# A chain of Mamba, window and convolution layers on one core: the output y written over the conv's output, and three of twelve products with B moved to GpSimd in the second mixer stage

## The chip, the cores and the metric

One core of one Trainium2 chip runs the whole program in one launch. The metric is the device time of that launch in microseconds (us). Engines are named as in the profile: PE (TensorE matmul), PEld (its weight loads), DVE (VectorE), ACT (ScalarE), POOL (GpSimd), SP (SyncE, which issues nearly all DMAs).

## What is computed

An image batch of 4 x 192 x 64 x 64 in float32 goes through four layers. Layer 0 is a norm and two Mamba mixers (the second on flipped channels), added to the norm's output. Layer 1 is a norm, one Mamba mixer, a depthwise 3x3 conv with a GELU and an MLP. Layers 2 and 3 are a masked conv with generated weights and a window layer with two projections. The change concerns the mixers of layers 0 and 1 alone. A mixer, cut from the reference:

```python
xc, z = split(x @ in_w.T)
xc = silu(causal_conv(xc) + conv_b)
dt, B, C = split(xc @ x_w.T)
dt = softplus(dt @ dt_w.T + dt_b)
# for each step t, channel d (384) and state n (16):
h = exp(dt * A) * h + (dt * xc) * B
y = sum_n(h * C)
out = ((y + D * xc) * silu(z)) @ out_w.T
```

## The kernel before

**Stages.** `two_mambas` computes layer 0 (the first stage): 32 tiles of 512 tokens, each with two mixers m0 and m1, so 64 mixer tiles. `mamba_block` computes layer 1 (the second stage): 32 mixer tiles of 512 tokens with one mixer (`summed=True`), and beside them, on the same engines, the output projection, the depthwise conv, a norm and the MLP of earlier tiles. `conv_and_windows` follows.

**The scan.** A mixer tile has 12 groups k of 4 scan steps j, 48 steps in all. A group covers 4 x 128 rows (16 channels times 8 states each) by 512 tokens. For a group:

- SP loads dt and dt*xc, spread over the states, from DRAM to `dtE` and `dtxE` (`load`, L588), a pair of groups at a time and 8 or 12 steps ahead.
- The **product** with B (L616 to 626): h = dtxE * B, 128 x 2048 elements. B lies spread in a PSUM bank of its own (`spread`, L597), which DVE reads. [...] In the first stage `shared` is (3, 7, 11) for m0 and (2, 5, 8, 11) for m1. In the second it is empty.
- ACT makes the decay dA = exp(dt * A), one 128 x 512 per step, two steps ahead, in three PSUM banks (`decay`, L628).
- DVE scans (`step`, L634, L636).
- POOL copies the last column to `state` and multiplies h by C (`read`, L645 to 651), issued after the group's last step.
- PE sums over the states with a gather matrix, four 32-column matmuls side by side (`sum`, L653), some steps later.

After every third of the groups, `skip` and `gate` (L677 to 691) make y = (ys + D * xc) * silu(z). In the first stage D * xc is added by one more matmul (`skip_w`) and DVE multiplies by z. In the second DVE adds D * xc and POOL multiplies. y is a tile of its own, one per mixer, and the out projection in `back` reads it.

**What sets the order.** All instructions are put in order by hand, on the host. `Scans.run` goes through the steps of all tiles in a row. A step issues its loads, the decay of two steps later, its own scan, and at the group's end the read with C and the next product (L741 to 785); a shared product is issued six steps ahead of its first scan (L761). Sums, skips and gates fall due a fixed number of steps later (L776). After each step `behind.tick` adds the work that runs beside the scans. This work stands in lanes (`Behind`, L175): generators that yield a `Piece` with the PE time of the next piece, the ticks to wait, what must have been issued before, and whether it needs one of two PSUM banks. A tick gives 1.6 (first stage) or 1.8 (second) of PE time. An ACT copy out of a bank is put off by `later` for one or two ticks, a DVE read by two or three. A `burst` is a long ACT function that needs another table than the decay's exp (Silu, Softplus, Gelu): it goes out only at an **edge** (L737), one per edge, and an edge is a tick before a group whose product DVE makes. `force` (L270) issues everything until a condition holds, for example `"rows" in u` before the first load of a next tile (L751).

In the second stage a tile has five bursts: Silu of xc (L488), Softplus of dt (L512), Silu of z (L530), Gelu of the conv branch (L1136) and Gelu of the MLP (L388). Lane 1 holds the front half (in projection, taps, dt, z) of the next tile and then the norm of the one after it; lane 0 the spread of C and `back`; lanes 2 and 3 the conv, the second norm and the MLP.

Of the kernel before, what the change touches and what calls it, by code (L numbers as in the profile page):

```python
# [22 lines left out]
C = 192  # L23
# [151 lines left out]
class Behind:  # L175
# [7 lines left out]

    def __init__(self, psum, tile, act, dve, spare, lanes=4):
# [234 lines left out]
class Mamba:  # L419
# [3 lines left out]
    def __init__(  # L423
        self, nc, name, taps, ins, const, last, scan, work, psum_y, psum_a, dram, ident, ex, behind, shared=(),
        summed=False,
    ):

        self.behind, self.y_free, self.shared, self.summed = behind, True, shared, summed  # L430
# [24 lines left out]
        if shared:  # L455
            self.skip_w = scan.tile([128, ND, 128], F32, name=f"{name}_skip")
            for d in range(ND):
                nc.vector.tensor_scalar_mul(self.skip_w[:, d, :], ident, self.D[:, d : d + 1])
        self.halo = scan.tile([128, ND, taps if summed else taps - 1], F32, name=f"{name}_halo")
        self.state = scan.tile([128, NQ, 4], F32, name=f"{name}_state")  # L460

    def front(self, xn, first, u):
# [28 lines left out]
        for d in range(ND):  # L491
            nc.tensor.matmul(ps, self.x_w[:, d, :], xc[:, d, :], start=(d == 0), stop=(d == ND - 1))  # L492
        dbl = u["dbl"] = self.work.tile([RK + 2 * NS, T], F32, name="dbl", bufs=2)
        h = behind.later(lambda ps=ps: nc.scalar.copy(dbl, ps))  # L494
# [29 lines left out]
        for d in range(ND):  # L524
            if d:
                yield Piece(1.7, bank=True)
            made.append(project(ND + d, z[:, d, :]))
        u["xn_read"] = True
        yield Piece(after=made, burst=True, act=4.1)
        nc.scalar.activation(z, z, AF.Silu)  # L530
        u["silu"] = True

    def convolve(self, raw, project, u):
# [6 lines left out]
        for d in range(ND):  # L540
            for j in range(K):
                if j % 2 == 0:
                    yield Piece(1.7 if j < K - 1 else 0.85, bank=j == 0, after=made + u["xc_free"])
                if d == j == 0:
                    xc = u["xc"] = self.work.tile([128, ND, T], F32, name="xc", bufs=3)
                if j == 0:
                    ps = behind.bank([128, T], "ps_conv")
                nc.tensor.matmul(  # L548
                    ps, self.conv[:, d, j, :], raw[:, d, j : j + T], start=(j == 0), stop=(j == K - 1)
                )  # L550
# [10 lines left out]
    def sum_taps(self, raw, projected, u):  # L561
# [3 lines left out]
        for d in range(ND):  # L565
            yield Piece(1.7, bank=True, after=u["xc_free"])
            if d == 0:
                xc = u["xc"] = self.work.tile([128, ND, T], F32, name="xc", bufs=3)
                one = self.work.tile([128, ND, 1 + T], F32, name="one", tag="dt", bufs=1)
# [27 lines left out]
    def spread(self, u, o):  # L597

        B = u["B", o] = self.psum_a.tile([128, T], F32, name=f"B{o}", bufs=1)
        self.nc.tensor.matmul(B, self.ex.spread[:, o, :], u["dbl"], start=True, stop=True)  # L600

    def spread_C(self, u, o):

        for n, i in (("C", 2 + o), ("Bs", o)):
            if n == "Bs" and not any(k % 2 == o for k in self.shared):
                return
            if n == "Bs":
                yield Piece(0.85, bank=True)
# [44 lines left out]
    def sum(self, u, k):  # L653
# [3 lines left out]
        for j in range(4):  # L657
# [4 lines left out]
                start=(i == 0),  # L662
                stop=(i == 3 and not self.shared),
                skip_group_check=bool(self.shared),
            )
        if i == 3 and self.shared:
            c = k // 4
# [9 lines left out]
    def skip(self, u, c):  # L677
        if c == 0:
            u["y"] = self.last.tile([128, ND, T], F32, name=f"{self.name}_y", bufs=1)
        if self.shared:  # L680
            self.nc.vector.tensor_tensor(u["y"][:, c, :], u["ys"], u["z"][:, c, :], ALU.mult)
            return
        self.nc.vector.scalar_tensor_tensor(
            u["y"][:, c, :], u["xc"][:, c, :], self.D[:, c : c + 1], u["ys"], ALU.mult, ALU.add
        )

    def gate(self, u, c):
        if self.shared:
            return
        y = u["y"][:, c, :]  # L690
        self.nc.gpsimd.tensor_tensor(y, y, u["z"][:, c, :], ALU.mult)


class Scans:
# [6 lines left out]
    def __init__(self, nc, units, behind):  # L701
        self.nc, self.units, self.behind = nc, units, behind
        self.due = {}
        for n, unit in enumerate(units):
            unit[1]["skipped"], unit[1]["gated"] = [False], [False]
            unit[1]["xc_free"] = [units[n - 3][1]["skipped"]] if n > 2 else []
            unit[1]["z_free"] = [units[n - 2][1]["gated"]] if n > 1 else []
# [8 lines left out]
    def run(self):  # L716
# [3 lines left out]
        for o in range(2):  # L720
            m.spread(u, o)
            self.behind.add(0, m.spread_C(u, o), Piece(0.85, bank=True))
        for i in range(2):
# [17 lines left out]
    def step(self, i, n):  # L741
# [24 lines left out]
        if j == 3:  # L766
            self.behind.force(lambda: ("C", k % 2) in u)
            m.read(u, k)
            if k >= NQ - 2 and i + 8 < n:
                m2, u2, _, _ = self.tile(i + 8)  # L770
                self.behind.add(0, m2.spread_C(u2, k - (NQ - 2)), Piece(0.85, bank=True))
# [19 lines left out]
    def skip(self, m, u, c):  # L791
        self.behind.force(lambda: "silu" in u)
        if c == 0:
            self.behind.force(lambda: m.y_free)
            m.y_free = False
        m.skip(u, c)
        u["skipped"][0] = c == ND - 1

# [5 lines left out]
def two_mambas(tc, x, gb_ap, m_ins, ex_aps, out, at_first):  # L804
# [3 lines left out]
    with ExitStack() as ctx:  # L808
# [16 lines left out]
            Mamba(  # L825
                nc, f"m{i}", 4, m_ins[i], const, work, const, work, psum_y, psum_a, dram, ident, ex, behind, ((3, 7, 11), (2, 5, 8, 11))[i]
            )
# [51 lines left out]
        def back(u):  # L879
            o = work.tile([128, nq, C], F32, name="o", bufs=2)  # L880
            made = []
            for q in range(nq):
                yield Piece(2.6, bank=True, wait=0 if q else 2)
                ps = behind.bank([128, C], "ps_out")
                for i in range(2):
                    for d in range(ND):
                        nc.tensor.matmul(
                            ps,
                            u[i]["y"][:, d, bass.ts(q, 128)],
                            mambas[i].out_w[:, d, :],  # L890
# [13 lines left out]
                made.append(behind.later(lambda q=q, ps=ps: nc.scalar.copy(o[:, q, :], ps)))  # L904
            mambas[0].y_free = mambas[1].y_free = True
            yield Piece(after=made)
# [91 lines left out]
def mamba_block(tc, x, p96, p96_ap, p128, p128_ap, m_in, ex_aps, out, sums, following):  # L998
# [4 lines left out]
    with ExitStack() as ctx:  # L1003
# [57 lines left out]
        def back(u):  # L1061
# [13 lines left out]
            for k in range(2):  # L1075
                yield Piece(2.6, bank=True, wait=0 if k else 3)
                ps = behind.bank([CP, T], "ps_out")
                for d in range(ND):
                    nc.tensor.matmul(
                        ps,  # L1080
                        mamba.out_w[:, d, bass.ts(k, CP)],
                        u["m"]["y"][:, d, :],
                        start=(d == 0),
# [12 lines left out]
                )  # L1096
            mamba.y_free = True
            yield Piece(after=made)
# [734 lines left out]
```

## Time and profile before

| | us |
|---|---|
| three runs | 10616.35, 10621.16, 10621.92 (median 10621.16) |
| the profiled execution | 10617.22 |
| its span, first to last instruction | 10615.4 |
| first scan and last scan of the first stage, start | 77.4, 5236.6 |
| first scan and last scan of the second stage, start | 5337.7, 8693.0 |
| product with B on DVE (L623), mean | 2.262 |
| product with B on POOL (L623), mean | 4.645 |
| read with C on POOL (L649), mean | 4.533 |
| one scan (L636), mean | 1.267 |
| ACT copy of C or Bs (L612), median | 0.584, 0.586 |
| an ACT table load | 1.283 |

How to read it: the profile is one execution of the program. An engine's time is busy when one of its instructions runs; the idle time before an instruction is put down to what ended last before it started (the releaser). A mean over the whole program mixes the stages, so the views by stretch of time say more. The granted clock is the share of full speed at which PE was allowed to run; matmuls take longer where it is low.

### The profile page before, as it was taken

What the parts mean: (1) busy time and instruction counts of PE and PEld (TensorE: products, weight loads), DVE (VectorE), ACT (ScalarE), POOL (GpSimd) and SP (SyncE); (2) the same over time, 40 slices, a digit from 0 to 9 for tenths busy, and PEclk for the clock granted to TensorE, in tenths of its full rate; (3) what the DMA queues carried; (4) which work ended last, traced back from release to release, by engine and by line L of the source; (5) the groups of instructions that cost most, each with busy time, mean ns of one, the idle gap of its engine ahead of it and who ended that gap; (6) DMA issues with size and microseconds to landing.
All of it is one profiled execution on the core that took longest, in us unless ns stands there. A gap on an engine that the chain in (4) does not pass through costs nothing. (4 is left out here: it accounts for less than half of the span.)

```text
span 10615.4 us, 97365 instructions
## 1 busy us (share of the span) xinstructions
PE 8816.2 (83%) x30840; PEld 3533.1 (33%) x30840; DVE 8979.4 (85%) x7665; ACT 6664.2 (63%) x9658; POOL 7510.6 (71%) x3616
## 2 busy tenths in 40 slices
PE   6887887887877888888569999999999986889899
PEld 2322222322322322322223333333333333545555
DVE  7999999999999999999788888888888876555552
ACT  5676776667676767767456676767676653434433
POOL 6999999999999999999767777777777651111100
PEclk7888888888888888888668888898988887999999
DMA  6666666666666666666455555555555542122110
GB/s 167 172 185 182 179 182 186 179 179 185 182 181 183 182 181 183 183 182 179 132 147 142 140 143 141 143 141 147 141 143 141 142 103 73 45 52 60 44 41 18
DMA packets 969561, 1515.12 MB, mean 143 GB/s; under 512 B 244346, under 2 KB 277150, under 8 KB 968534
## 3 DMA queue, kind: packets, MB, share of 16 engines
q1 hardware_dynamic: 968190, 1505.85, 53.2%
q8 instruction: 244, 4.00, 0.2%
q10 hardware_dynamic: 856, 3.05, 0.1%
q14 instruction: 271, 2.22, 0.1%
HBM read 1295.45 MB, written 213.12 MB: 142 GB/s over the span
## 5 line engine op out<-in xcount | busy, mean ns | idle before, releaser
L636 DVE TENSOR_TENSOR_SCAN h<-dA,m_state,h 128x512 f32<-128x512 f32 x3712 | 4518.1, 1267 | 340.8 <-ACT dA L630 262.3
L649 POOL TENSOR_TENSOR h<-h,C 128x2048 f32<-128x2048 f32 x928 | 4206.4, 4533 | 75.1 <-POOL m_state L648 0.6
L630 ACT ACTIVATE dA<-dtE,m_A 128x512 f32<-128x512 f32 x4608 | 3105.4, 687 | 1446.1 <-DVE h L636 1328.3
L623 DVE TENSOR_TENSOR h<-dtxE,B 128x2048 f32<-128x2048 f32 x928 | 2099.0, 2262 | 78.0 <-DMA dtxE<-r_dtx 68.5
L658 PE MATMUL y<-h,gather 128*32 128x512 f32 x7424 | 1160.8, 701 | 462.0 <-POOL h L649 338.2
L1368 POOL TENSOR_TENSOR d<-d,rs 128x512 f32<-128x512 f32 x64 | 86.3, 1349 | 1597.1 <-DVE rs L1367 1576.5
L636 DVE TENSOR_TENSOR_SCAN h_apart<-dA,m_state,h_apart 128x512 f32<-128x512 f32 x896 | 1079.3, 1260 | 63.5 <-ACT dA L630 55.1
L474 PE MATMUL ps_in<-xT,m_in_w 96*128 96x512 f32 x1536 | 917.2, 746 | 244.6 <-ACT o L904 154.1
L623 POOL TENSOR_TENSOR h_apart<-dtxE,Bs 128x2048 f32<-128x2048 f32 x224 | 1040.5, 4645 | 10.0 <-ACT Bs L612 10.0
L649 POOL TENSOR_TENSOR h_apart<-h_apart,C 128x2048 f32<-128x2048 f32 x224 | 1014.6, 4529 | 18.0
L648 POOL COPY m_state<-h 128x4 f32<-128x4 f32 x928 | 176.8, 191 | 888.8 <-DVE h L636 883.8
L548 PE MATMUL ps_conv<-raw,m_conv 128*128 128x512 f32 x1536 | 724.2, 608 | 7.2 <-ACT raw L481 6.0
L474 PEld LDWEIGHTS ps_in<-xT,m_in_w 96*128 96x128 f32 x1536 | 357.9, 243 | 839.3 <-issue 373.3
L1117 PE MATMUL ps_dw<-strip,dw 96*96 96x512 f32 x1152 | 588.4, 660 | 3.3 <-ACT x L1126 0.9
L474 PE MATMUL ps_in<-xn,m_in_w 96*128 96x512 f32 x768 | 443.1, 721 | 164.4 <-ACT z L481 70.6
L658 PEld LDWEIGHTS y<-h,gather 128*32 128x32 f32 x7424 | 156.3, 115 | 1175.8 <-issue 580.9
L503 PE MATMUL ps_dt<-dbl,m_dt_w 12*128 12x512 f32 x576 | 410.4, 824 | 156.1 <-ACT dbl L494 99.5
L395 PE MATMUL ps_o<-hid,t 128*96 128x512 f32 x768 | 449.9, 733 | 78.7 <-ACT ln_rs L332 66.8
L1533 PE MATMUL sed_ps<-xn,sed 64*128 64x256 f32 (+3 forms) x2944 | 486.0, 404 | 7.0 <-DVE y L1552 7.0
L492 PE MATMUL ps_x<-xc,m_pack 128*44 128x512 f32 x576 | 357.6, 771 | 142.8 <-ACT xc L488 133.7
L630 ACT ACT_TABLE_LOAD x345 | 442.6, 1283 | 14.8 <-DMA dtE<-r_dt 8.6
L513 POOL TENSOR_TENSOR raw<-dt,xc 128x1536 f32<-128x1536 f32 x96 | 325.0, 3385 | 166.0 <-ACT dt L512 129.6
(202 smaller groups left out, 12347.7 us busy)
## 6 DMA issues: line engine op xcount, KB each, us to landing
dtE<-r_dt SPq DMA_DIRECT2D x2304, 256.0 KB, 5.2
dtxE<-r_dtx SPq DMA_DIRECT2D x2304, 256.0 KB, 4.2
r_dt<-dt SPq DMA_DIRECT2D x96, 768.0 KB, 4.0
r_dtx<-raw SPq DMA_DIRECT2D x96, 768.0 KB, 6.5
x<-x SPq DMA_DIRECT2D x64, 384.0 KB, 3.9
img<-x SPq DMA_DIRECT2D x28, 512.0 KB, 8.1
xt<-in_x SPq DMA_DIRECT2D x32, 384.0 KB, 5.4
x<-o SPq DMA_DIRECT2D x32, 384.0 KB, 3.9
```

The lines of the kernel that those rows point to most:

```text
L395: nc.tensor.matmul(ps, self.w2[:, m, bass.ts(k, CP)], h[:, m, :], start=(m == 0), stop=(m == NH - 1),)
L474: nc.tensor.matmul(ps, self.in_w[:, k, bass.ts(e, 128)], xn[:, k, :], start=(k == 0), stop=(k == 1))
L492: nc.tensor.matmul(ps, self.x_w[:, d, :], xc[:, d, :], start=(d == 0), stop=(d == ND - 1))
L503: nc.tensor.matmul(ps, self.dt_w[:, bass.ts(d, 128)], dbl[:RK, :], start=True, stop=True)
L548: nc.tensor.matmul(ps, self.conv[:, d, j, :], raw[:, d, j : j + T], start=(j == 0), stop=(j == K - 1))
L623: engine.tensor_tensor(h, u["rows", k // 2, 1], u[B, k % 2].unsqueeze(1).broadcast_to([128, 4, T]), ALU.mult)
L630: self.nc.scalar.activation(dA, u["rows", k // 2, 0][:, j, :], AF.Exp, scale=self.A[:, k, j : j + 1])
L636: self.nc.vector.tensor_tensor_scan(h[:, j, :], u.pop(("dA", k, j)), h[:, j, :], self.state[:, k, j : j + 1], ALU.mult, ALU.add,)
L649: nc.gpsimd.tensor_tensor(h, h, u["C", k % 2].unsqueeze(1).broadcast_to([128, 4, T]), ALU.mult)
L658: self.nc.tensor.matmul(u["ys"][32 * j : 32 * j + 32, :], self.ex.gather[:, i // 2, :], h[:, j, :], start=(i == 0), stop=(i == 3 and not s ...
L1117: nc.tensor.matmul(ps, dw[:, k, j, :], s[:, k, dy : dy + rows, dx : dx + HW], start=(j == 0), stop=(j == 8),)
L1533: nc.tensor.matmul(out, sed[p, int(h is not None), i ^ position(k, s), cols], xn[b, g][p, c, :], start=group(t) not in begun, stop=left[gr ...
```

## The change

In the mixers of both stages:

- y is no tile of its own: `skip` and `gate` write over xc, and the out projection reads xc. xc now lies in the pool of longer life (`last`), with three buffers in the second stage as before and four in the first (`xcs`). Instead of `skipped` and `y_free`, a flag `y_read` frees the buffer once the out projection is issued.
- `dbl` has one buffer instead of two.
- `Bs` is copied by ACT from B's own PSUM bank; the second matmul for it is gone.

In the second stage alone:

- `shared` is (3, 7, 11): POOL makes three of twelve products, into one `h_apart` buffer. With that, the ticks before groups 3, 7 and 11 are no edges.
- `spread_C` makes Bs first and C second for odd groups; for even groups C has one buffer and its matmul waits three ticks.
- Silu of z moves from lane 1 into a lane 4 of its own.
- The sum of groups 1, 5 and 9 comes one step later.

The core of the diff:

```diff
-        dbl = u["dbl"] = self.work.tile([RK + 2 * NS, T], F32, name="dbl", bufs=2)
+        dbl = u["dbl"] = self.work.tile([RK + 2 * NS, T], F32, name="dbl", bufs=1)
...
-        u["xn_read"] = True
-        yield Piece(after=made, burst=True, act=4.1)
-        nc.scalar.activation(z, z, AF.Silu)
-        u["silu"] = True
+        def silu():
+            nc.scalar.activation(z, z, AF.Silu)
+            u["silu"] = True
+            yield Piece()
+        said = Piece(after=made, burst=True, act=4.1)
+        if self.summed:
+            behind.add(4, silu(), said)
+        else:
+            yield said
+            yield from silu()
...
-                    xc = u["xc"] = self.work.tile([128, ND, T], F32, name="xc", bufs=3)
+                    xc = u["xc"] = self.last.tile([128, ND, T], F32, name="xc", bufs=self.xcs)
...
+    def alone(self, o):
+        return self.summed and o == 0
     def spread_C(self, u, o):
-        for n, i in (("C", 2 + o), ("Bs", o)):
-            if n == "Bs" and not any(k % 2 == o for k in self.shared):
-                return
-            if n == "Bs":
-                yield Piece(0.85, bank=True)
-            v = self.work.tile([128, T], F32, name=f"{n}{o}", bufs=2 if n == "C" else 1)
-            ps = self.behind.bank([128, T], f"ps_{n}")
-            self.nc.tensor.matmul(ps, self.ex.spread[:, i, :], u["dbl"], start=True, stop=True)
-            done = self.behind.later(lambda v=v, ps=ps: self.nc.scalar.copy(v, ps))
+        both = [("Bs", 0, 1)] if any(k % 2 == o for k in self.shared) else []
+        both.insert(len(both) if self.summed else 0, ("C", 2 + o, 1 if self.alone(o) else 2))
+        for n, i, bufs in both:
+            if n == "C":
+                yield Piece(0.85, bank=True, wait=3 * self.alone(o))
+            v = self.work.tile([128, T], F32, name=f"{n}{o}", bufs=bufs)
+            if n == "C":
+                ps = self.behind.bank([128, T], f"ps_{n}")
+                self.nc.tensor.matmul(ps, self.ex.spread[:, i, :], u["dbl"], start=True, stop=True)
+            else:
+                ps = u["B", o]
+            done = self.behind.later(
+                lambda v=v, ps=ps: self.nc.scalar.copy(v, ps), bank=(n == "C")
+            )
             yield Piece(after=[done])
             u[n, o] = v
...
-            h = self.work.tile([128, 4, T], F32, name="h_apart", bufs=2)
+            h = self.work.tile([128, 4, T], F32, name="h_apart", bufs=1 if self.summed else 2)
...
     def skip(self, u, c):
-        if c == 0:
-            u["y"] = self.last.tile([128, ND, T], F32, name=f"{self.name}_y", bufs=1)
-        if self.shared:
-            self.nc.vector.tensor_tensor(u["y"][:, c, :], u["ys"], u["z"][:, c, :], ALU.mult)
+        y = u["xc"][:, c, :]
+        if not self.summed:
+            self.nc.vector.tensor_tensor(y, u["ys"], u["z"][:, c, :], ALU.mult)
             return
-        self.nc.vector.scalar_tensor_tensor(
-            u["y"][:, c, :], u["xc"][:, c, :], self.D[:, c : c + 1], u["ys"], ALU.mult, ALU.add
-        )
+        self.nc.vector.scalar_tensor_tensor(y, y, self.D[:, c : c + 1], u["ys"], ALU.mult, ALU.add)
...
-            unit[1]["xc_free"] = [units[n - 3][1]["skipped"]] if n > 2 else []
+            xcs = unit[0].xcs
+            unit[1]["xc_free"] = [units[n - xcs][1]["y_read"]] if n >= xcs else []
...
-            added, skipped, gated = (7, 10, 10) if m.shared else (4, 6, 8)
-            if m.shared and k % 4 == 0:
-                added += 2
+            added, skipped, gated = (4, 6, 8) if m.summed else (7, 10, 10)
+            if k % 4 == 0 and not m.summed or k + 2 in m.shared and m.summed:
+                added += 1 if m.summed else 2
...
         mamba = Mamba(
-            nc, "m", 3, m_in, const, work, fixed, scan, psum_y, psum_a, dram, ln.ident, ex, behind, summed=True
+            nc, "m", 3, m_in, const, work, fixed, scan, psum_y, psum_a, dram, ln.ident, ex, behind, (3, 7, 11), True
         )
```

More of the change, by code (lines that the diff above doesn't have):

```diff
@@ L182, with __init__ @@
     BANKS = 2
-    def __init__(self, psum, tile, act, dve, spare, lanes=4):
+    def __init__(self, psum, tile, act, dve, spare, lanes=5):
         self.psum, self.tile, self.act, self.dve = psum, tile, act, dve
@@ L424, in __init__ @@
         self, nc, name, taps, ins, const, last, scan, work, psum_y, psum_a, dram, ident, ex, behind, shared=(),
-        summed=False,
+        summed=False, xcs=3,
     ):
-        self.behind, self.y_free, self.shared, self.summed = behind, True, shared, summed
+        self.behind, self.xcs, self.shared, self.summed = behind, xcs, shared, summed
         self.nc, self.name, self.taps, self.ex = nc, name, taps, ex
@@ L454, in __init__ @@
                     )
-        if shared:
+        if not summed:
             self.skip_w = scan.tile([128, ND, 128], F32, name=f"{name}_skip")
@@ L567, in sum_taps @@
             if d == 0:
-                xc = u["xc"] = self.work.tile([128, ND, T], F32, name="xc", bufs=3)
+                xc = u["xc"] = self.last.tile([128, ND, T], F32, name="xc", bufs=self.xcs)
                 one = self.work.tile([128, ND, 1 + T], F32, name="one", tag="dt", bufs=1)
@@ L662, in sum @@
                 start=(i == 0),
-                stop=(i == 3 and not self.shared),
-                skip_group_check=bool(self.shared),
+                stop=(i == 3 and self.summed),
+                skip_group_check=not self.summed,
             )
-        if i == 3 and self.shared:
+        if i == 3 and not self.summed:
             c = k // 4
@@ L677, in skip @@
     def skip(self, u, c):
-        if c == 0:
-            u["y"] = self.last.tile([128, ND, T], F32, name=f"{self.name}_y", bufs=1)
-        if self.shared:
-            self.nc.vector.tensor_tensor(u["y"][:, c, :], u["ys"], u["z"][:, c, :], ALU.mult)
+        y = u["xc"][:, c, :]
+        if not self.summed:
+            self.nc.vector.tensor_tensor(y, u["ys"], u["z"][:, c, :], ALU.mult)
             return
-        self.nc.vector.scalar_tensor_tensor(
-            u["y"][:, c, :], u["xc"][:, c, :], self.D[:, c : c + 1], u["ys"], ALU.mult, ALU.add
-        )
+        self.nc.vector.scalar_tensor_tensor(y, y, self.D[:, c : c + 1], u["ys"], ALU.mult, ALU.add)
     def gate(self, u, c):
-        if self.shared:
+        if not self.summed:
             return
-        y = u["y"][:, c, :]
+        y = u["xc"][:, c, :]
         self.nc.gpsimd.tensor_tensor(y, y, u["z"][:, c, :], ALU.mult)
@@ L704, in __init__ @@
         for n, unit in enumerate(units):
-            unit[1]["skipped"], unit[1]["gated"] = [False], [False]
-            unit[1]["xc_free"] = [units[n - 3][1]["skipped"]] if n > 2 else []
+            unit[1]["y_read"], unit[1]["gated"] = [False], [False]
+            xcs = unit[0].xcs
+            unit[1]["xc_free"] = [units[n - xcs][1]["y_read"]] if n >= xcs else []
             unit[1]["z_free"] = [units[n - 2][1]["gated"]] if n > 1 else []
@@ L721, in run @@
             m.spread(u, o)
-            self.behind.add(0, m.spread_C(u, o), Piece(0.85, bank=True))
+            self.behind.add(0, m.spread_C(u, o), Piece())
         for i in range(2):
@@ L770, in step @@
                 m2, u2, _, _ = self.tile(i + 8)
-                self.behind.add(0, m2.spread_C(u2, k - (NQ - 2)), Piece(0.85, bank=True))
+                o = k - (NQ - 2)
+                self.behind.add(0, m2.spread_C(u2, o), Piece())
             if i + 1 < n:
@@ L792, in skip @@
         self.behind.force(lambda: "silu" in u)
-        if c == 0:
-            self.behind.force(lambda: m.y_free)
-            m.y_free = False
         m.skip(u, c)
-        u["skipped"][0] = c == ND - 1
     def sum(self, m, u, k):
@@ L825, in two_mambas @@
             Mamba(
-                nc, f"m{i}", 4, m_ins[i], const, work, const, work, psum_y, psum_a, dram, ident, ex, behind, ((3, 7, 11), (2, 5, 8, 11))[i]
+                nc, f"m{i}", 4, m_ins[i], const, work, const, work, psum_y, psum_a, dram, ident, ex, behind,
+                ((3, 7, 11), (2, 5, 8, 11))[i], xcs=4,
             )
@@ L888, in back @@
                             ps,
-                            u[i]["y"][:, d, bass.ts(q, 128)],
+                            u[i]["xc"][:, d, bass.ts(q, 128)],
                             mambas[i].out_w[:, d, :],
@@ L904, in back @@
                 made.append(behind.later(lambda q=q, ps=ps: nc.scalar.copy(o[:, q, :], ps)))
-            mambas[0].y_free = mambas[1].y_free = True
+            u[0]["y_read"][0] = u[1]["y_read"][0] = True
             yield Piece(after=made)
@@ L1081, in back @@
                         mamba.out_w[:, d, bass.ts(k, CP)],
-                        u["m"]["y"][:, d, :],
+                        u["m"]["xc"][:, d, :],
                         start=(d == 0),
@@ L1096, in back @@
                 )
-            mamba.y_free = True
+            u["m"]["y_read"][0] = True
             yield Piece(after=made)
```

## The prediction

> **What bounds the kernel now.** First the page: span, busy times, and three rows of its 40 slices (one slice is 265 us).
>
> ```profile
> span 10615.4 us, 97365 instructions
> PE   6887887887877888888569999999999986889899
> DVE  7999999999999999999788888888888876555552
> POOL 6999999999999999999767777777777651111100
> ```
>
> Three stages show: the two mixers up to slice 19, the single mixer (the "second stage") up to slice 32, the windows after it. DVE and POOL are full in the first; in the second PE is fullest, DVE is at 8 and POOL at 7. The change works in the first two. Next the busy time by stretch (after the width: PE, PEld, DVE, ACT, POOL, then the granted clock), one steady stretch of each:
>
> ```profile
> 600.00:5100.00 4500.00, 3626.72 (x11713) 1300.86 (x11712) 4359.55 (x3341) 3153.15 (x4839) 4296.38 (x1827) 0.83 0.67 182
> 5600.00:8600.00 3000.00, 2716.29 (x8246) 968.85 (x8247) 2656.07 (x2071) 2064.78 (x2750) 2125.76 (x1165) 0.88 0.53 142
> ```
>
> The second stretch holds 1363 scans, 48 to a tile, so 28.4 tiles of 105.6 us. Per tile DVE is busy 2656/28.4 = 93.5 us and idle 12.1, PE busy 95.6, ACT 72.7, POOL 74.9. What ends DVE's idle time there (total us, times, longest):
>
> ```profile
> DVE h L636 <- ACT dA L630: 179.4, 151, 7.0
> DVE x L1152 <- PE ps_o L395: 80.8, 54, 4.1
> DVE xn L347 <- PE rb L339: 45.1, 29, 3.4
> ```
>
> The last two are PE directly. The first is ACT, and ACT's own waits in that stretch, apart from those for DVE, are for PE: 139 us for C's matmul, 120 for ps_dw, 106 for ps_h, 69 for z. So DVE waits because PE is late. Last, PE by pieces of one tile:
>
> ```profile
> 6941.00:6955.00 14.00, 13.72 (x42) 4.18 (x43) 13.44 (x11) 8.60 (x15) 9.76 (x6) 1.00 0.65 169
> 6955.00:6962.00 7.00, 7.00 (x15) 1.61 (x14) 6.90 (x6) 4.10 (x5) 5.94 (x3) 0.53 0.55 145
> 6962.00:6976.00 14.00, 12.08 (x39) 3.98 (x37) 10.56 (x8) 10.73 (x14) 11.50 (x5) 0.99 0.84 255
> 6976.00:6983.00 7.00, 6.49 (x8) 2.73 (x9) 4.46 (x5) 4.20 (x7) 3.52 (x4) 0.52 0.07 16
> 6983.00:7000.00 17.00, 16.69 (x67) 6.73 (x65) 16.06 (x13) 14.79 (x18) 10.57 (x5) 0.99 0.46 123
> 7000.00:7010.00 10.00, 7.78 (x13) 2.60 (x10) 9.90 (x7) 8.38 (x12) 7.60 (x5) 0.50 0.56 144
> ```
>
> The granted clock is 1.0 or 0.5, and three stretches of together 24 us in this tile have the half clock: about 12 us of PE's 95.6. The second stage is held by PE and DVE together: PE busy 90%, DVE 88%.
>
> **The change, part by part.**
>
> *Three products from DVE to POOL, second stage.* The price on either engine stands in the first stage, where POOL makes such products already:
>
> ```profile
> 4940.73 4.79 DVE L636 TENSOR_TENSOR_SCAN h_apart<-dA,m_state,h_apart 128x512 f32<-128x512 f32 x4
> 4945.43 2.26 DVE L623 TENSOR_TENSOR h<-dtxE,B 128x2048 f32<-128x2048 f32 x1
> ...
> 4952.52 2.26 DVE L623 TENSOR_TENSOR h<-dtxE,B 128x2048 f32<-128x2048 f32 x1
> ```
>
> A group of four scans whose product POOL made takes DVE 4945.43 - 4940.73 = 4.70 us; with the product 4952.52 - 4945.43 = 7.09. So 2.39 us fall away, 3 x 2.39 = 7.17 per tile, 32 x 7.17 = **229 us** in all, if DVE sets the end everywhere. The scans beside POOL's products last 1.26 us as elsewhere, so POOL's reading costs DVE nothing.
>
> POOL gets 3 x 4.645 = 13.9 us per tile: 74.9 + 13.9 = 88.8. Is there room? The products are queued at scan steps 6, 22 and 38 of a tile, ahead of the next read with C:
>
> ```profile
> 6922.51 1.01 POOL L333 TENSOR_TENSOR ln_rs<-ln_rs,minus_half 128x4 f32<-128x4 f32 x1 [4.44 <-ACT ln_rs L332]
> 6955.52 0.19 POOL L648 COPY m_state<-h 128x4 f32<-128x4 f32 x1 [3.31 <-DVE h L636]
> 6992.69 0.19 POOL L648 COPY m_state<-h 128x4 f32<-128x4 f32 x1 [5.00 <-DVE h L636]
> ```
>
> POOL is idle 4.44, 3.31 and 5.00 us at just these places, so 4.65 us delay what follows by 0.2, 1.3 and 0. Each product is due six steps later, over 10 us off in this trace. I count POOL at 0; were its idle time gone, the reads with C would be late and PE's gather sums behind them, at most 13.9 us a tile. [...]
>
> How much of 7.17 stays? The savings fall before steps 12, 28 and 44. After the first two, the next thing in DVE's queue that waits is at steps 30 to 35 (0.88, 1.54, 0.91 and 2.54 us, all for dA, whose ACT queue stood behind ps_dw and ps_h); after the third it is the next tile's norm and ps_o. From 6942 to 6976, steps 15 to 32, PE waits for nothing. If that stretch stays as it is, DVE only arrives earlier and waits longer: 0 is kept. That is the lower end. The upper end is 7.17. Between them stands a row of this stage: its second tile (first scans at 5437.93 and 5535.55, 97.6 us), where PE does no conv and no MLP yet and is busy 64.65 of 97 us. It is 8 us shorter than a steady tile, so about two thirds of DVE's idle time is PE's doing and the rest is DVE's own pace. I take **half**, 3.6 us x 32 = 115 us, the middle of ends for which no row decides. Below nothing is possible too, through the next part.
>
> *Bursts.* ACT's long functions with a table load go only to a tick before a DVE product, so groups 3, 7 and 11 are no longer offered: nine places for five bursts. Softplus now goes at 6959.76 (step 25, ahead of group 7) and the MLP's Gelu at 6996.93 (step 41, ahead of group 11); both go four steps later, and the Gelu of the conv branch and the Silu of z make room. z's Silu has a lane of its own and no longer holds the next norm. 0, hidden by slack: dt and dtx must be in DRAM by step 36, softplus at 29 needs some 4 us of ACT, 3.3 of POOL, and the wait of two ticks. If that cover is gone it costs a whole burst, 1.28 + 1.48 + 1.28 = 4.0 us of ACT a tile.
>
> *Bs and C.* Second stage: one more ACT copy a tile, 0.58 x 32 = 18.6 us, behind which the dA's stand; ACT now waits up to 4.72 us there for C's matmul (6911.13), so the copy fits in: between 0 and 18.6, I take 0. C0 has one buffer, its copy is three ticks later and waits for POOL's read of group 10; if POOL lags, dA stands behind it. First stage: Bs comes from B's bank, 3 x 32 = 96 matmuls of about 1.1 us leave PE, and ACT's wait for them (24.6 us in the stretch above). DVE's idle time there is 4500 - 4360 = 140 us, 46 of it at the h_apart scans behind ps_conv, not behind Bs. Between 0 and 25; I take **5**, since DVE and POOL are full (97 and 95%) anyway.
>
> *y in xc, dbl and h_apart single, xc of four.* No instruction more or less. dbl is rewritten at steps 11 to 18, its last reader ends by step 3: 0. y's buffer is free when the out projection has read it, long before a fourth tile: 0. h_apart is rewritten at step 22 after the sum issued at 19, which ends at 6951.3, before POOL is free at 6952.2: 0, else some 2 us of POOL.
>
> **Sum**: the profiled execution took 10617.2 us (span 10615.4): 10617.2 - 115 - 5 = 10497. The median of the runs shown is 4 above that execution, so I say **10500**.
>
> [...]
>
> **Rivals.**
> 1. *DVE sets the pace everywhere.* All of 229 + 5 is kept: 10383. [...] Against: 305 us of DVE's waits are PE's. 0.12.
> 2. *PE is the bound, DVE waits instead.* Nothing kept but the first stage's few us: about 10610. It also covers a POOL that turns out late. For: PE waits for nothing over 34 us of the tile. Against: the order of PE's work shifts with the bursts. 0.17.
> 3. *Slower: softplus misses step 29.* With dt's evacuations late by more than four steps (they end at step 23 now), the next place is step 33, and at step 36 the loader forces everything out off its place. It decides from the point where the front half starts four steps later, since z now comes after the later softplus. Price: nothing kept, and 4.0 us of ACT burst uncovered per tile, 32 x 4.0 = 128: 10745. With half of the savings kept: 10630. 0.14.
> 4. *Forecast*: part is kept, 10430 to 10590. 0.57.
>
> Measurement can tell about 0.2%, 21 us, from no change. Faster by more: all of 4, 1 and a little of 2, 0.71; within: most of 2, 0.14; slower: rival 3 and a remainder, 0.15. The range takes in part of 1 and the mild form of 3: 10390 to 10640.
>
> **What would show it.** Right: 96 products at L623's line on POOL in the second stage at 4.6 us; DVE busy down to about 86.7 us a tile, tiles of 101 to 103 us, DVE's idle share up a little, POOL near 88 us a tile, softplus four steps later; the first stage within 10 us. Rival 1: tiles of 98.5 us and PE's clock above 0.92. Rival 2: tiles of 105 us, DVE's wait for dA grown by some 200 us. Rival 3: a table load right at step 36 with DVE idle after it. Wrong in kind would be a wait of DVE for POOL's products, or of ACT for POOL at C0's copy.

## The result, and the profile after

The changed kernel takes **10560.1 us** (median of 4 runs, 10558.9 to 10570.0) against 10618.8 before (median of 4, 10615.0 to 10621.9): ratio 0.9947, 95% interval 0.9930 to 0.9964. It is faster by 0.53%, as forecast in sign and inside the range, but with 59 us instead of 121 it gained a little less than half.

The page of the changed kernel, the rows that answer to those of before:

```profile
span 10559.3 us, 96732 instructions
PE   6777777877877777787668888888888996889898
DVE  7999999999999999999878887887888876555552
POOL 6999999999999999999778887888888861101100
```

In the second stage POOL rose from 7 to 8 and DVE fell by less than a tenth. The same two stretches as before (the second ends 100 us earlier; columns: width, PE, PEld, DVE, ACT, POOL, clock, DMA):

```profile
600.00:5100.00 4500.00, 3551.78 (x11570) 1271.37 (x11571) 4364.89 (x3346) 3155.56 (x4843) 4299.48 (x1828) 0.83 0.67 182
5600.00:8500.00 2900.00, 2589.72 (x8033) 930.76 (x8030) 2401.72 (x1934) 2015.88 (x2701) 2435.95 (x1222) 0.90 0.53 142
```

DVE is idle 498 of 2900 us, 17%, where it was 344 of 3000, 11%. What ends that idle time:

```profile
DVE h_apart L654 <- ACT dA L648: 124.5, 75, 6.1
DVE h L654 <- ACT dA L648: 124.1, 134, 4.4
DVE strip L1102 <- PE ps_out L1093: 116.6, 55, 5.4
DVE xn L309 <- PE mean L307: 65.1, 53, 4.0
```

There is no wait for POOL's products. DVE does its part sooner and waits longer for PE and for ACT behind PE. Where the time went, from the two profiled executions: the first stage, first scan to last, 5160.5 to 5150.1 us (-10.4); the second 3356.6 to 3325.6 (-31.0); what follows the last scan 1921.2 to 1908.8 (-12.4); the rest some 2 us.

The tiles of the second stage show something that no mean does. From first scan to first scan, before: 105.8 us for most tiles, with 103.4 and 104.7 for the first two of an image. After: 102.4 for most, but 111.4 and 113.4 for the third and fourth of an image. Eight tiles together: 843.1 us before, 839.7 after. So the steady tile is 3.4 us shorter, and the two long ones give nearly all of that back. The first scans of two tiles in a row after the change, 102.42 us apart:

```profile
6572.15 4.81 DVE L654 TENSOR_TENSOR_SCAN h<-dA,m_state,h 128x512 f32<-128x512 f32 x4 [1.46 <-ACT dA L648]
...
6674.57 2.46 DVE L654 TENSOR_TENSOR_SCAN h<-dA,m_state,h 128x512 f32<-128x512 f32 x2 [1.45 <-ACT dA L648]
```

**A long tile and its neighbour.** The two tiles that begin at 6458.7 and 6572.15 us hold the same instructions in the same order on PE, DVE, ACT and POOL, and yet:

```profile
6458.70:6572.10 113.40, 100.99 (x292) 34.57 (x292) 87.12 (x70) 73.15 (x99) 88.21 (x45) 0.85 0.49 132
6572.10:6674.60 102.50, 91.49 (x292) 32.66 (x292) 86.93 (x71) 73.42 (x100) 88.29 (x45) 0.93 0.55 146
```

DVE, ACT and POOL are busy for the same time; PE needs 9.5 us more, at a clock of 0.85 against 0.93. PE's waits sum to about 11 us in either. Its longest ones in the long tile:

```profile
PE y L676 <- POOL h_apart L667: 3.6, 1, 3.6
PE ps_in L475 <- ACT z L482: 1.9, 1, 1.9
PE ps_o L395 <- ACT C L629: 1.8, 1, 1.8
```

and in the short one:

```profile
PE ps_o L395 <- ACT C L629: 3.2, 1, 3.2
PE ps_in L475 <- ACT z L482: 1.9, 1, 1.9
PE y L676 <- POOL h_apart L667: 1.9, 1, 1.9
```

What differs is where the half clock falls. The stretches at half clock, in the long tile (three more of its windows are at its start):

```profile
6499.50:6506.50 7.00, 5.25 (x12) 1.02 (x13) 7.00 (x8) 4.34 (x5) 6.92 (x4) 0.53 0.33 95
6517.00:6530.50 13.50, 13.50 (x22) 3.52 (x22) 7.44 (x6) 8.80 (x11) 6.17 (x3) 0.50 0.14 44
6544.20:6547.60 3.40, 3.40 (x5) 1.32 (x5) 2.93 (x3) 0.89 (x3) 3.40 (x4) 0.51 1.04 267
```

in the short one (the third row is the start of the tile behind it; at its own start two windows, 6571.6 to 6578.4, have the half clock likewise):

```profile
6595.50:6598.80 3.30, 3.30 (x5) 1.02 (x5) 0.75 (x1) 2.24 (x4) 3.22 (x3) 0.50 0.04 9
6626.20:6629.60 3.40, 3.40 (x5) 1.14 (x4) 2.65 (x3) 0.45 (x1) 3.24 (x4) 0.50 1.07 265
6674.00:6680.80 6.80, 4.47 (x5) 1.46 (x6) 6.23 (x5) 4.11 (x8) 4.10 (x4) 0.50 0.02 5
```

In the traces before and after, the clock changes only on one grid of 3.4133 us, to within 1 ns over some 3000 windows, through all stages. One step of this grid is called a clock window here. Now divide the steady tiles by that window: before 105.81 / 3.413 = **31.0**, after 102.41 / 3.413 = **30.0**, in the longer runs of equal tiles to within 0.02. The loop of the second stage runs in step with the clock windows. Equal tiles in a row begin at the same place of a window (0.05 to 0.06 of it before, 0.16 to 0.17 after) and have their half-clock windows at the same places: from 51.0, 54.4, 71.5, 74.9, 95.4, 98.8 and 102.2 us behind a tile's first scan before, from -0.6, 2.8, 23.3 and 54.0 us after. What puts the half clock there, no run tests. A tile that begins elsewhere in a window (0.93 of it in place of 0.16) got other half-clock windows and another length. The steady tile's own 3.4 us show in the same records: 7 of its 31 windows had the half clock before (the 24 us that the prediction lists), 4 of 30 after, and PE's busy time fell from 95.6 to 91.5 us.

So the theory taken to the chip: in the second stage PE and its clock set the tile, DVE's load hardly matters, the order of work decides on which whole number of windows the loop settles, and a tile with another order throws it out of step. The rival: DVE's relief is what gained, and something else, the moved bursts, the double conv branch at an image's end or the new lane, costs half of it.

### The profile page after: what moved, and what is told of

It is laid out like the page before. It is cut to its first block, busy times and chain, and to the rows that moved or that the text cites. A ratio compares the mean times of both kernels' runs of the same rounds, so it can differ in the third digit from the quotient of the medians.

```text
span 10559.3 us, 96732 instructions
## 1 busy us (share of the span) xinstructions
PE 8657.5 (82%) x30648; PEld 3478.9 (33%) x30648; DVE 8765.6 (83%) x7569; ACT 6675.7 (63%) x9690; POOL 7932.4 (75%) x3712
## 5 line engine op out<-in xcount | busy, mean ns | idle before, releaser
L654 DVE TENSOR_TENSOR_SCAN h<-dA,m_state,h 128x512 f32<-128x512 f32 x3328 | 4041.4, 1266 | 269.8 <-ACT dA L648 207.8
L667 POOL TENSOR_TENSOR h<-h,C 128x2048 f32<-128x2048 f32 x832 | 3768.3, 4529 | 71.3 <-ACT C L629 4.0
L641 DVE TENSOR_TENSOR h<-dtxE,B 128x2048 f32<-128x2048 f32 x832 | 1881.7, 2262 | 74.5 <-DMA dtxE<-r_dtx 68.1
L654 DVE TENSOR_TENSOR_SCAN h_apart<-dA,m_state,h_apart 128x512 f32<-128x512 f32 x1280 | 1551.2, 1262 | 199.9 <-ACT dA L648 190.0
L641 POOL TENSOR_TENSOR h_apart<-dtxE,Bs 128x2048 f32<-128x2048 f32 x320 | 1475.5, 4611 | 35.2 <-ACT dA L648 16.2
L667 POOL TENSOR_TENSOR h_apart<-h_apart,C 128x2048 f32<-128x2048 f32 x320 | 1449.7, 4530 | 25.8
L676 PE MATMUL y<-h,gather 128*32 128x512 f32 x6656 | 1040.1, 701 | 486.9 <-POOL h L667 311.5
L676 PE MATMUL y<-h_apart,gather 128*32 128x512 f32 x2560 | 397.8, 698 | 178.7 <-POOL h_apart L667 169.9
L475 PE MATMUL ps_in<-xn,m_in_w 96*128 96x512 f32 x768 | 403.1, 660 | 114.8 <-ACT z L482 61.7
L395 PE MATMUL ps_o<-hid,t 128*96 128x512 f32 x768 | 418.5, 684 | 70.5 <-ACT C L629 63.7
```

The costliest lines, as they stand in the source:

```text
L395: nc.tensor.matmul(ps, self.w2[:, m, bass.ts(k, CP)], h[:, m, :], start=(m == 0), stop=(m == NH - 1),)
L475: nc.tensor.matmul(ps, self.in_w[:, k, bass.ts(e, 128)], xn[:, k, :], start=(k == 0), stop=(k == 1))
L641: engine.tensor_tensor(h, u["rows", k // 2, 1], u[B, k % 2].unsqueeze(1).broadcast_to([128, 4, T]), ALU.mult)
L654: self.nc.vector.tensor_tensor_scan(h[:, j, :], u.pop(("dA", k, j)), h[:, j, :], self.state[:, k, j : j + 1], ALU.mult, ALU.add,)
L667: nc.gpsimd.tensor_tensor(h, h, u["C", k % 2].unsqueeze(1).broadcast_to([128, 4, T]), ALU.mult)
L676: self.nc.tensor.matmul(u["ys"][32 * j : 32 * j + 32, :], self.ex.gather[:, i // 2, :], h[:, j, :], start=(i == 0), stop=(i == 3 and self. ...
```

## The experiments

**1. The room alone.** The change with its second-stage part undone: `shared` empty there, z's Silu in lane 1, two buffers for C0.

```diff
-            ... ln.ident, ex, behind, (3, 7, 11), True
+            ... ln.ident, ex, behind, (), True
...
-        return self.summed and o == 0
+        return False
...
-        if self.summed:
-            behind.add(4, silu(), said)
-        else:
-            yield said
-            yield from silu()
+        yield said
+        yield from silu()
```

> The change without its second-stage part: y over xc, one dbl, Bs copied from B's bank in the first stage; in the second stage no product on POOL, z's Silu in lane 1, C as before. Own theory (the second stage runs in step with PE's clock windows of 3.413 us: 31 windows a tile before, 30 after, and falls out of step for two tiles per image after): first stage some 11 us shorter as in the changed kernel, second stage at 31 windows (105.8 us) as before, total some 10 to 25 us below the kernel before. Rival (the room and y's place are the gain, POOL's products bring nothing): total near the changed kernel, 55 us below.

Measured 10596.5 us (9 runs, 10575.6 to 10600.3), ratio 0.9974 (0.9965 to 0.9984): 22 us gained, as its own theory had it. The profiled execution is the shortest of these runs. In it the first stage took 5148.3 us, 12 less than before, and the first seven tiles of the second stage took 711.9 us in place of 723.6. Steady tiles are 105.8 us in the second and last image; in the third, tiles of some 103.8 and 104.4 us alternate, two of them 208.3 us or 61.0 windows. What follows the last scan is no shorter (1922.1 us; 1921.2 before). So about 22 of the 59 us are the room and Bs's copy, some 36 the second-stage part.

**2. Twelve products on DVE, twelve edges.** The changed kernel with `shared` empty in the second stage, nothing else.

> The changed kernel with no product on POOL in the second stage, so that all twelve ticks are edges again; lane 4, the single C and dbl stay. Own theory: DVE gets 7.2 us a tile back, the steady tile is a whole number of clock windows again, 31 (105.8 us) or 32 (109.2), total 0 to 100 us above the changed kernel. Rival (the two slow tiles per image come from lane 4 and the later C, not from the products or the moved bursts): the two slow tiles of 111 and 113 us stay.

Measured 11047.1 us (4 runs), ratio 1.0407 (1.0391 to 1.0422). Far worse than either theory said: the steady tile is 126.3 us (37.0 windows), and in the trace DVE waits some 10 us at step 38 of a tile.

**3. The old edges.** POOL's products stay, but bursts may also go ahead of groups 3, 7 and 11.

```diff
-        return i % 4 == 3 and (i + 1 >= n or self.tile(i + 1)[2] not in self.tile(i + 1)[0].shared)
+        return i % 4 == 3 and (i + 1 >= n or self.tile(i + 1)[0].summed or self.tile(i + 1)[2] not in self.tile(i + 1)[0].shared)
```

> The changed kernel with edges before groups 3, 7 and 11 too, so that softplus and the MLP's Gelu go out where they did before, without a DVE product beside them. Own theory: the order of PE's work, not DVE's load, sets the tile: it goes back to 31 windows (105.8 us) or to another whole number, and ACT's bursts of 4 us stand open at three groups; total 0 to 100 us above the changed kernel. Rival (the later bursts are what costs half of the gain): total below the changed kernel by up to 110 us.

Measured 11114.3 us (4 runs), ratio 1.0467 (1.0450 to 1.0485), most tiles of 128 to 132 us, again worse than either theory said. With lane 4 and the early edges, the work fits together no longer: Silu of xc goes out at step 29 in the steady tiles, where it is 13 before and 17 after the change, and softplus misses its places. Then the loader of the next tile, at step 36, forces out what is left. ACT in that stretch of one tile:

```profile
6728.60 1.30 ACT L648 ACTIVATE dA<-dtE,m_A 128x512 f32<-128x512 f32 x2
6732.91 0.69 ACT L507 ACTIVATE dt<-ps_dt,m_pack 128x512 f32<-128x512 f32 x1 [3.01 <-PE ps_dt L504]
6734.81 0.69 ACT L507 ACTIVATE dt<-ps_dt,m_pack 128x512 f32<-128x512 f32 x1 [1.21 <-PE ps_dt L504]
6737.35 0.69 ACT L507 ACTIVATE dt<-ps_dt,m_pack 128x512 f32<-128x512 f32 x1 [1.86 <-PE ps_dt L504]
6738.06 1.28 ACT L513 ACT_TABLE_LOAD   x1
6739.35 1.48 ACT L513 ACTIVATE dt<-dt 128x1536 f32<-128x1536 f32 x1
6740.86 1.28 ACT L648 ACT_TABLE_LOAD   x1
6742.15 0.69 ACT L648 ACTIVATE dA<-dtE,m_A 128x512 f32<-128x512 f32 x1
```

Three copies of dt out of PSUM, each waiting for its matmul, and softplus with both table loads stand together with no dA between them; DVE waits 10.16 us for the dA at 6742.15. This is the third rival of the prediction. The changed kernel escapes it.

**4. Even tails.** The conv branch of an image's last tile is queued one tile later, so that each tile queues one and none queues two.

```diff
-            for t2 in ([t - 1] if t else []) + ([t] if t == NT - 1 else []):
-                behind.add(2, tail(b, t2), Piece(2.6, bank=True, after=first, wait=2))
+            for n2 in ([n - 1] if n else []) + ([n] if n == len(units) - 1 else []):
+                behind.add(2, tail(*divmod(n2, NT)), Piece(2.6, bank=True, after=first, wait=2))
```

> The changed kernel with the conv branch of an image's last tile queued one tile later, so that every tile queues just one and the order of work is the same for all tiles past the start. Own theory: nothing throws the second stage out of step, nearly all tiles take 30 windows (102.4 us), the two tiles of 111.4 and 113.4 us per image are gone: 18 to 20 us for each of three or four images, total 45 to 80 us below the changed kernel. Rival (the slow tiles come from the image's start itself, the memsets and the work of two conv branches): they stay, total within 10 us of the changed kernel.

Measured **10498.5 us** (4 runs, 10493.1 to 10501.3), ratio 0.9890 (0.9875 to 0.9905). From the eighth tile on all but the last take 102.4 us; the tiles of 111.4 and 113.4 are gone. This is 62 us below the changed kernel, inside what the own theory said, and the shortest time of a kernel that does the whole work.

**5. The same in the kernel before.**

> The kernel before with the conv branch of an image's last tile queued one tile later, the same edit that took 60 us from the changed kernel. Own theory (the steady tile is a whole number of PE's clock windows and any change of the order throws it off): here the tiles out of step were the short ones (103.4 and 104.7 us against 105.8), so they vanish too and the kernel becomes 3 x 3.5 = some 10 us slower. Rival (two conv branches in one tile are simply bad): it becomes faster by 20 us or more.

Measured 10618.7 us (10 runs), ratio 0.9998 (0.9989 to 1.0008). Neither came true: the tiles of 103.4 and 104.7 us stay. There, what throws the loop out of step is not the doubled branch but something else, at an image's start; no run shows which memset or copy it is. Two tails in a row are not bad in themselves, though: they cost the kernel before nothing.

**6. and 7. Less work for DVE, nothing moved.** Scans of the second stage over 448 of 512 columns (the last 64 are left out), on the kernel of 4 and on the kernel before.

```diff
-            h[:, j, :],
-            u.pop(("dA", k, j)),
-            h[:, j, :],
+            h[:, j, :n],
+            u.pop(("dA", k, j))[:, :n],
+            h[:, j, :n],
```

> The changed kernel with even tails and second-stage scans over 448 of 512 columns: the scan of the last 64 columns is left out, which takes some 0.14 us from each of 48 scans, 6.5 to 7 us of DVE a tile, about as much as the three products, with no instruction moved. Own theory (PE and its clock set the tile, DVE waits): the steady tile stays at 30 windows (102.4 us) or falls by one at most (99.0); DVE's idle time grows by what it saves. Rival (DVE sets half of the pace or all): the tile falls by 3.5 to 7 us off any whole number of windows, total 110 to 220 us lower.

> The kernel before with second-stage scans over 448 of 512 columns (the rest left out): DVE loses 6.5 to 7 us a tile, as with the change, but nothing goes to POOL and no edge moves. Own theory: the steady tile stays at 31 windows (105.8 us) or falls to 30 (102.4), so the gain is 0 or about 109 us. Rival (DVE's own pace is half or all of it): tiles of 102.3 or 99, and everything between is possible.

One run each: 10552.5 us on the kernel of 4, which is *longer* by 54, and 10606.3 on the kernel before, 14 below its median. The stretch 6500 to 8500, first the kernel of 4, then 6:

```profile
6500.00:8500.00 2000.00, 1786.42 (x5684) 635.82 (x5683) 1692.99 (x1364) 1433.14 (x1910) 1719.97 (x859) 0.93 0.55 147
```

```profile
6500.00:8500.00 2000.00, 1811.10 (x5552) 637.99 (x5551) 1530.86 (x1335) 1390.37 (x1864) 1676.82 (x840) 0.89 0.54 142
```

then the kernel before, and 7:

```profile
6500.00:8500.00 2000.00, 1811.87 (x5530) 642.87 (x5529) 1775.10 (x1387) 1382.16 (x1838) 1422.74 (x781) 0.89 0.53 142
```

```profile
6500.00:8500.00 2000.00, 1812.95 (x5497) 642.87 (x5498) 1647.21 (x1376) 1369.15 (x1833) 1406.35 (x773) 0.88 0.54 142
```

In 7 DVE is busy 128 us less out of 2000, and PE's busy time and clock stay. Most tiles are still 105.8 us: a tile with some 6.5 us less of DVE takes as long as one with it. What changed lies elsewhere: the first seven tiles, before the loop is in step, took 698.7 us in place of 723.6, so there a lighter DVE may count, and some tiles at an image's start were longer (109.1 us). In 6 the loop is out of step, tiles of 101 to 111 us, with the clock at 0.89; neither theory had that. DVE's pace doesn't set the steady tile.

**8. Less work for PE.** Two of the nine taps of the depthwise conv left out, on the kernel of 4.

```diff
                     dy, dx = divmod(j, 3)
+                    if j in (2, 5):
+                        continue
```

> The changed kernel with even tails and seven of the nine taps of the depthwise conv: two taps (four matmuls a tile, 3.4 us of PE at full clock, 6.8 at half) are left out, DVE, ACT and POOL keep their work. Own theory: PE sets the pace, the tile falls by at least one window (to 99.0 us or less), total 100 us lower or more. Rival (DVE or POOL sets the pace): the tile stays at 102.4 us.

One run: 10455.8 us, 43 below the kernel of 4, where 100 or more were expected. The tile falls, but not by a window: it goes 102.0, 99.4, 102.0, 101.8, 100.0, and over again. Those five are 505.2 us, 148.0 windows; the loop is in step over five tiles instead of one. The stretch shown above for 4:

```profile
6500.00:8500.00 2000.00, 1793.57 (x5604) 631.43 (x5604) 1714.55 (x1388) 1438.07 (x1926) 1741.39 (x868) 0.90 0.56 148
```

The half clock now takes 6 windows a tile in place of 4, so PE is busy 90.6 us a tile in place of 91.5, although two taps are left out, an estimated 3.6 us at full clock (three taps take 5.39 us there in the changed kernel). The tile gains 1.4 us. PE's work counted here where DVE's didn't, but this is one run, in another step with the clock.

**9. and 10. The order without POOL's products.** Everything of the change stays in place, the edges too, but DVE makes the products of groups 3, 7 and 11, from B's bank, when it used to (POOL's products read `Bs`, a copy of B in SBUF); on the changed kernel and on that of 4.

```diff
-        engine, B = (self.nc.gpsimd, "Bs") if apart else (self.nc.vector, "B")
+        engine, B = (self.nc.gpsimd, "Bs") if apart and not self.summed else (self.nc.vector, "B")
...
-                m2.product(u2, k2)
+                if not m2.summed:
+                    m2.product(u2, k2)
...
-                if k2 not in m2.shared:
+                if k2 not in m2.shared or m2.summed:
                     m2.product(u2, k2)
```

> The changed kernel with everything in its new place (edges, lane 4, Bs, C, sums), but the products of groups 3, 7 and 11 made by DVE in their old place, from B's bank. It tells the order apart from the work that left DVE. Own theory (PE and its clock set the steady tile, DVE idles 15 us of 102): DVE takes 7.2 us a tile more and mostly fills its idle time; steady tiles of 102.4 or 105.8 us, total 0 to 60 us above the changed kernel. Rival (the relief of DVE is what the second stage gained): tiles 7 us longer, total over 150 us above the changed kernel.

> The same with even tails: DVE makes all twelve products, the order is the one that stays in step. Own theory: steady tiles of 30 windows (102.4 us) or 31 (105.8), total 0 to 100 us above the changed kernel with even tails. Rival (DVE's relief is the gain): tiles of 107 us or more, total over 150 us above it.

Measured 10568.0 us, ratio 0.9948 (0.9931 to 0.9964), where the changed kernel has 0.9947; and 10504.6, ratio 0.9888 (0.9873 to 0.9903), where the kernel of 4 has 0.9890. The medians differ by 8 and 6 us, the ratios to the kernel before by nothing. **The three products on GpSimd bring nothing that can be told from the spread of the runs.** The steady tile is 102.4 us with or without them, and the long tiles of 111.4 and 113.4 us are in 9 as in the changed kernel. In 10, against the 1692.99 us of DVE shown above for 4:

```profile
6500.00:8500.00 2000.00, 1787.01 (x5682) 636.26 (x5681) 1820.98 (x1424) 1436.92 (x1915) 1458.31 (x798) 0.93 0.55 146
```

DVE does 128 us more in the same time, and PE's columns are the same to 1 us. Where these 128 us were: DVE's waits over the stretch in 4,

```profile
DVE h_apart L654 <- ACT dA L648: 103.0, 59, 3.6
DVE strip L1102 <- PE ps_out L1093: 82.1, 38, 3.6
```

and in 10:

```profile
DVE strip L1103 <- PE ps_out L1094: 36.8, 38, 1.2
...
DVE h_apart L654 <- ACT dA L648: 14.8, 21, 1.4
```

103.0 - 14.8 + 82.1 - 36.8 = 133.5 us of waiting become work. With the products on POOL, DVE reached groups 3, 7 and 11 early and waited there for dA and for ps_out, which came no sooner.

**11. and 12. Without lane 4.** z's Silu in lane 1 again, on the changed kernel and on that of 4 (the third part of the edit of 1).

> The changed kernel with z's Silu in lane 1 again, so that the next norm waits for that burst. Theory: lane 4 is needed because the bursts go four steps later; without it the norm and then the front half start later, softplus misses step 29 and the loader forces the rest out at step 36, as in the two kernels with twelve edges: tiles over 110 us, total above the kernel before. Rival: lane 4 makes no difference that counts, total within 30 us of the changed kernel.

> The same with even tails, to see the steady tile of that order for itself. Theory: tiles over 110 us as in the other. Rival: tiles of a whole number of windows between 102.4 and 109.2 us.

One run each: 10972.0 and 10971.6 us, steady tiles of 119 to 120 us (four of them 140.0 windows), as the theory said. Lane 4 is needed with the new edges, as the new edges are needed with lane 4 (2 and 3). Either alone costs 410 to 550 us against the changed kernel.

## Where the prediction was right, and the step that failed

- **Price of the products**: right. 96 more on POOL, 4.61 us on the mean of both stages; DVE 86.9 us a tile in the steady tile, 86.7 foreseen.
- **POOL's idle gaps**: right. POOL is busy 88.3 us a tile, 88.8 foreseen, and DVE waits for no product. PE waits 1.9 us a tile for a read with C of a shared group.
- **"I take half, 3.6 us x 32 = 115 us"**: this step failed. Nothing of DVE's 7.17 us is kept in the steady tile (7, 9, 10); the lower end of its bounds was the truth. The row that was to stand between the ends, a tile of 97.6 us with little work for PE, was read as a third of DVE's idle time being DVE's own pace. That reading was wrong too: DVE is busy 89.6 us in that tile, 93.5 in a steady one, so half of the 8 us was work that DVE doesn't have there, and its idle time fell only from 12.1 to 8.0. Outside the steady tiles the products' relief isn't shown to pay either. The last tile takes 89.5 us with them on POOL and 95.5 in 9 and 10, but what follows the last scan then takes 6.0 us more (1908.8 against 1902.8). The second tile takes 93.5 us against 98.1 in 9 and 97.5 in 10, but 94.1 in 1, which has no products on POOL. That the steady tile is 3.4 us shorter, close to 3.6, is chance: it is one clock window.
- **Bursts at 0**: also wrong, in both directions. They went four steps later as said, softplus from step 25 to 29, and Silu of xc too, from 13 to 17. The new order made the steady tile one window shorter (9 and 10 have it without the products). It brought the second-stage part's 36 us, and would have brought 98 with even tails (1 against 4). And it is close to orders that cost over 400 us (2, 3, 11).
- **First stage, 5 us**: 10.4 in the profiled execution, inside 0 to 25.
- **Rival 2** (PE is the bound, DVE waits instead) had the mechanism; its time of 10610 lacked the effect of the order, which it named without a size. Rival 3's forced front half was real, in neighbours of the changed kernel. Rival 1 is out. Of the some 12 us a tile that the half clock cost PE before (half of 24 us), the new order gave back 4.1 (95.6 to 91.5 us of PE a tile).
- **Not foreseen**: the loop in step with the clock, the two long tiles per image (9.0 + 11.0 us, which nearly cancel what six tiles gain), and 12.4 us after the last scan, which come with the second-stage part (1 has none of them, 9 and 10 have 18).

So the 59 us are 22 of the room and Bs's copy and some 36 of the order; the products' 115 did not come. What stays open: which of the moved pieces makes 30 windows out of 31, and what starts the short tiles of an image in the kernel before.

## What to carry to other kernels

Before an engine is relieved, ask whether its waits are its own: here the three rows behind DVE's idle time (PE twice, and ACT, which itself waited for PE) were the answer, and 115 us were still booked. A cheap test is to shorten that engine's instructions in place, with nothing moved, and see whether the loop gets shorter; since that can put the loop out of step, as in 6, give the engine its work back in the new order too, as in 9 and 10. And where a hand-made order serves several engines, a change of the work moves the order too: measure the order without the work, and look at the iterations one by one, since a mean hides that some are long.

## What the runs showed of the hardware

- In this loop, PE busy some 90%, the steady tile was a whole number of PE's clock windows: 31.00 windows of 3.413 us a tile (before, 5, 7), 30.00 with another order (after, 4, 9, 10), 37.0 in 2, 140.0 for four tiles in 11 and 12, 148.0 for five in 8. In 3 and 6 the tiles are less regular. In step, some 6.5 us of DVE work more or less a tile changed nothing in the steady tile (7 against before, 10 against 4). Out of step, the same instructions took 113.4 instead of 102.4 us (after).
- Two matmuls of ps_dw in a row start 0.43 us apart at the full clock and 0.85 us at the half one (medians, before and after). The half clock came without long gaps of PE. In the steady tile after the change, before two of its half-clock windows (from 6595.5 and 6626.2 us) PE was busy 2.90 and 2.62 of the window's 3.41 us, its longest waits 0.35 and 0.78 us, beside matmuls with one column (var) and with 12 rows (ps_dt). Before a full-clock window in the same tile (from 6592.1 us) it was busy only 2.35 us, with a wait of 1.06. So the idle share alone did not decide; what did, no run shows. Some 4 of 30 windows run at half clock in the good tile and 10 of 33 in the long one.
- Scans on DVE with an operand in PSUM lasted 1.27 us beside POOL's products as without them (10 and 4).
